# A transformer block with gated delta rule: two levels of block products for gate and up of three batches, moved behind all delta rules

## The chip, the cores and the metric

The kernel runs on one core of one Trainium2 chip, all in fp32. The metric is device microseconds of one execution; lower is better. Three runs of the kernel before are at hand, and one execution was profiled.

## The reference

One adaLN block over x of 4 batches, 512 tokens and 512 channels:

```python
h = _layernorm(x) * (1 + ca) + sa
x = x + ga * attn(h)          # gated delta rule, 6 heads, key 64, value 128
h = _layernorm(x) * (1 + cb) + sb
x = x + gb * ffn(h)
# attn: q, k, v = silu(conv4(h @ W)); beta = sigmoid(h @ Wb); g = -exp(A) * softplus(h @ Wa + dt)
#       per token: S *= exp(g); S += k (v - k S) * beta; o = q S
#       then rmsnorm(o) * silu(h @ Wg) @ Wo
# ffn:  (silu(h @ w_gate.T) * (h @ w_up.T)) @ w_down.T,  512 -> 2048 -> 512
```

`sa, ca, ga, sb, cb, gb` come from a small product of the conditioning vector of each batch.

## The kernel before

One program, written as Python that emits instructions; a list scheduler then sets the order on each engine by priority (the order of emission, with some work put later by `tc.high_priority(-LATER)`). The stages per batch b:

- `normed_t`, `keys`, `queries`, `values`, `gates`: layer norm, transposes and projections (L424), with the convolutions. Batch 0 comes first by itself, the others together.
- `triangles(b)`: for each chunk of 64 tokens a triangular system is inverted. The 64x64 key products (L574) are weighted and stored in DRAM, come back as `pm` with one system to a partition, and DVE substitutes forward in 60 dependent operations (`tip` L598, `ti` L602). The inverses go out to DRAM again (`td`, `ttd`, L606 and L607), and `operands` (L609) loads them for the delta rule (L651 to L653).
- `delta_rule(b)`: four steps of `operands`, `scan` (L682, products L704), `finish` (L717), `project` (L735, L745) and `turned` (L759). `turned` makes the normalised, transposed input of the feed-forward (`hf`), by transposes into `pxn` and ACT. In this kernel `hf` stays in SBUF, two batches at a time.
- `feed_forward(b)` (L814). Tokens are split in halves, and so are channels, so that gate and up of a pair of feature blocks are 2x2 block products, made by seven products instead of eight: `two_blocks` (L947) with matmuls of 128x128 by 256 columns (L960) and sums by ACT and DVE (L965 to L974). The four differences of the tokens (`hs`) are made once in a batch on DVE, and the sums of the weights once for all batches by POOL in `weight_sums` (L794), into DRAM (`wsum`). Silu (L989) and the product with up (L990) give `hid`. A quarter is two such pairs, 512 of the 2048 features. Its down projection is direct (`down`, L842 and L847, 128x512; DVE multiplies by `gb`, L852, POOL adds to the residual, L853) or by seven products (`down_by_seven`, L871 and L890) in quarters 1 to 3 of batch 2 and 0 to 2 of batch 3: POOL makes the left factors (`left_factors`, L857), and the sums of the down weights (`dsum`) were made in feed-forward 1. `seven_to_output` (L903 to L931) ends a batch; its steps are let out one by one by `some`.

PSUM has banks `fill` (3) and `seq` (3). Loads go through SP's queue; DMA issues of one queue are in the order of the schedule. The stages around the change are emitted in this order:

```python
triangles(2)
feed_forward(0)
delta_rule(2)
triangles(3)
feed_forward(1)
delta_rule(3)
feed_forward(2)
feed_forward(3)
```

Since a feed-forward stands between the triangles and the delta rule that reads them, it runs beside the substitution on DVE. A quarter's down follows one pair later than its gate and up, and the last quarter of feed-forwards 0 to 2 is pending into the stage that follows.

Of the kernel before, what the change touches and what calls it, by code (L numbers as in the profile page):

```python
# [15 lines left out]
P = 128  # L16
# [6 lines left out]
S = 32  # L23
# [10 lines left out]
LATER = 4000  # L34


@with_exitstack
def adaln_block(
# [29 lines left out]
    w1 = ctx.enter_context(tc.tile_pool(name="w1", bufs=1))  # L68
    stage_b = ExitStack()
# [9 lines left out]
    def fill(name):  # L79
        return bank("fill", 3, name)  # L80
# [10 lines left out]
    def seq(name):  # L91
        return bank("seq", 3, name)


    kd, qd, vd, sd, gd, xmid = ([] for _ in range(6))
    for b in range(B):
        kd.append(dr.tile([P, NP, T], F32, name=f"kd{b}"))
        qd.append(dr.tile([P, NP, T], F32, name=f"qd{b}"))
        vd.append(dr.tile([NT, P, H, DV], F32, name=f"vd{b}"))
        sd.append(dr.tile([NT, DV, H, P], F32, name=f"sd{b}"))  # L100
        gd.append(dr.tile([2, 2, H, NT, C + 1], F32, name=f"gd{b}"))
        xmid.append(dr.tile([T, D], F32, name=f"xmid{b}"))
    wsum = [dr.tile([NF // 2, P, 7, 2, P], F32, name=f"wsum{i}") for i in range(2)]
# [109 lines left out]
    def load_x(b):  # L213
        ts = []
        if b == 2:

            room = w1.tile([P, NT, D], F32, tag="hf", bufs=2, name=f"xt{b}")
        for c in range(NT):
            if b == 2:
                t = room[:, c, :]  # L220
            else:
                t = pa_.tile([P, D], F32, tag="xt", bufs=4, name=f"xt{b}_{c}")
            (act if b else sp).dma_start(t, x[b, c * P : (c + 1) * P, :])
            ts.append(t)
        return ts
# [298 lines left out]
    ex, at, td, ttd, hf = {}, {}, {}, {}, {}  # L524

    def triangles(b):
# [9 lines left out]
        kp = w1.tile([P, NP, T], F32, tag="kp", bufs=1, name=f"kp{b}")  # L536
# [50 lines left out]
        pm = w1.tile([n, S, S], F32, tag="pm", name=f"pm_{b}")  # L587
        sp.dma_start(pm, ad)
        t = w1.tile([n, S, S], F32, tag="ti", name=f"ti_{b}")
        tmp = w1.tile([n, S * S // 4], F32, tag="tip", name=f"tip_{b}")  # L590
# [168 lines left out]
    def turned(b, c, xn):  # L759
        pt = seq(f"pxn{b}_{c}")  # L760
        for k in range(KD):
            pe.transpose(pt[:, k * P : (k + 1) * P], xn[:, k * P : (k + 1) * P], ident)
        for k in range(KD):
            act.activation(
                hf[b][:, k, c * P : (c + 1) * P], pt[:, k * P : (k + 1) * P], AF.Identity,
                bias=mod_t[:, 2, k, b : b + 1], scale=mod_t[:, 3, k, b : b + 1],
            )

    def delta_rule(b):
        ga = w1.tile([P, D], F32, tag="ga", name=f"ga{b}")  # L770
        sp.dma_start(ga, gate_d[0, b].partition_broadcast(P))
        hf[b] = w1.tile([P, KD, T], F32, tag="hf", bufs=2, name=f"hf{b}")
        st = operands(b, 0)
        for c in range(NT):
            nxt = operands(b, c + 1) if c + 1 < NT else None
            o = scan(b, c, st, nxt)
            finish(b, c, o, ga)
            st = nxt
# [35 lines left out]
    def feed_forward(b):  # L814
        nonlocal pd_

        own = pd_ if b == B - 1 else pc_
        gb = own.tile([P, D], F32, tag="gb", bufs=1, name=f"gb{b}")
        sp.dma_start(gb, gate_d[1, b].partition_broadcast(P))
        xm = []  # L820
        for c in range(NT):
            t = own.tile([P, D], F32, tag="xm", bufs=NT, name=f"xm{b}_{c}")
            sp.dma_start(t, xmid[b][c * P : (c + 1) * P, :])
            xm.append(t)
        ht = hf[b]
# [4 lines left out]
        if more is None:  # L830
            more = own.tile([P, 3, 2, TH], F32, tag="hs", bufs=1, name=f"hs{b}")
# [6 lines left out]
        tdn, acc, left = {}, {}, {}  # L838

        fast = {2: [1, 2, 3], 3: [0, 1, 2]}.get(b, [])  # L840
# [15 lines left out]

        def left_factors(q, j):  # L857

            hid = hids[q, j]
            a11, a12, a21, a22 = (  # L860
                hid[:, k, i * TH : (i + 1) * TH] for i in range(2) for k in range(2)
            )
            t = pd_.tile([P, 3, TH], F32, tag="sd", bufs=4, name=f"sd{b}_{q}_{j}")
            s1, s2, s4 = (t[:, k] for k in range(3))
            pool.tensor_add(s1, a21, a22)
            pool.tensor_sub(s2, s1, a11)
            pool.tensor_sub(a21, a11, a21)
            pool.tensor_sub(s4, a12, s2)
            left[q, j] = a11, a12, a22, a21, s1, s2, s4

        def down_by_seven(q):  # L871


            sums = {}
            for j in range(2):
                a11, a12, a22, a21, s1, s2, s4 = left[q, j]
                wd = wdn[q, j].rearrange("p j (h d) -> p j h d", h=2)
                d1, d2, d4, d3 = (tdn[q, j][:, k] for k in range(4))
                sums[j] = [
                    (a11, wd[:, 0, 0]), (a12, wd[:, 1, 0]), (s2, d2), (s1, d1), (a21, d3),  # L880
                    (s4, wd[:, 1, 1]), (a22, d4),
                ]
            if q == fast[0]:
                acc[0] = pd_.tile([P, 7, 2, 2 * P], F32, tag="acc", bufs=1, name=f"acc{b}")
            for k in range(7):
                o = fill(f"pds{b}_{q}_{k}").rearrange("p (c d) -> p c d", c=2)
                for c in range(2):
                    for j in range(2):
                        l, r = sums[j][k]
                        pe.matmul(o[:, c], l[:, c * P : (c + 1) * P], r, start=j == 0, stop=j == 1)  # L890
                if q == fast[0]:
                    act.copy(acc[0][:, k], o)
                else:
                    vec.tensor_add(acc[0][:, k], o, acc[0][:, k])

        def quarter(q):
            if q not in fast:
                return down(q)
            down_by_seven(q)
            if q == fast[-1]:  # L900
                ending.append(seven_to_output())

        def seven_to_output():  # L903

            p1, p2, p6, p5, p7, p3, p4 = (acc[0][:, k] for k in range(7))

            def add_to(tokens, k, v):
                ds = slice(k * TH, (k + 1) * TH)
                vec.tensor_tensor(v, v, gb[:, None, ds].broadcast_to([P, 2, TH]), ALU.mult)
                for c in range(2):  # L910
                    pool.tensor_add(xm[tokens + c][:, ds], xm[tokens + c][:, ds], v[:, c])

            vec.tensor_add(p6, p6, p1)
            vec.tensor_add(p1, p1, p2)
            yield
            vec.tensor_add(p7, p7, p6)
            add_to(0, 0, p1)
            yield
            vec.tensor_add(p2, p6, p5)
            vec.tensor_add(p2, p2, p3)  # L920
            yield
            vec.tensor_add(p4, p4, p7)
            add_to(0, 1, p2)
            yield
            vec.tensor_add(p5, p5, p7)
            add_to(2, 0, p4)
            yield
            add_to(2, 1, p5)
            if fast[-1] == NQ - 1:
                for i in range(NT):  # L930
                    sp.dma_start(out[b, i * P : (i + 1) * P, :], xm[i])  # L931

        def some(n):
            while ending and n:
                n -= 1
                if next(ending[0], 1):
                    ending.clear()
# [9 lines left out]
        def two_blocks(o, n, src, i):  # L947
# [6 lines left out]
            def product(l, r):  # L954
                count[0] += 1
                if count[0] % 2 == 0:
                    some(1)
# [18 lines left out]
        for i in range(0, NF, 2):  # L976
# [3 lines left out]
            wd = own.tile([P, 2, D], F32, tag="fwd", bufs=2, name=f"wdn{b}_{i}")  # L980
# [11 lines left out]
            if i == (0 if b == B - 1 else 2):  # L992
                complete()
                if b == 2:
                    stage_b.close()
                    pd_ = ctx.enter_context(
                        tc.tile_pool(name="pd", bufs=2, side="right", reuse_waits="tile")
                    )
            if b == 1:
# [9 lines left out]
            if q in fast:  # L1009
                tdn[q, j] = pd_.tile([P, 4, 2 * P], F32, tag="td", bufs=4, name=f"td{b}_{q}_{j}")  # L1010
                sp.dma_start(tdn[q, j], dsum[i // 2])
                left_factors(q, j)
            if j == 0 and q > 0:
                quarter(q - 1)
        if b == 2:
            pending.append(lambda: quarter(NQ - 1))
        else:
            some(9)
            quarter(NQ - 1)


    pd_ = None
    ending, count = [], [0]
# [38 lines left out]
    pc_ = ctx.enter_context(tc.tile_pool(name="pc", bufs=2, reuse_waits="tile"))  # L1062
# [6 lines left out]
    feed_forward(0)  # L1069
    delta_rule(2)  # L1070
    triangles(3)
    feed_forward(1)
    delta_rule(3)
    feed_forward(2)
    feed_forward(3)
# [45 lines left out]
```

## Time and profile before

| | us |
|---|---|
| median of 3 runs | 1312.97 |
| lowest, highest | 1311.42, 1314.52 |
| span of the profiled execution | 1315.2 |
| PE busy | 1234.9 (94%) |
| DVE busy | 733.7 (56%) |
| ACT busy | 383.5 (29%) |
| POOL busy | 290.8 (22%) |

The profiled execution is one of its own; its span stands 2.2 us above the median of the runs. In 40 slices of the span, each digit the tenths of it in which an engine is busy (PEclk: the granted clock of TensorE):

```profile
PE   6799898999889998999999999799999999999998
DVE  3665865656188255784445558543555543563564
POOL 4100214533210012030023121233111221131113
PEclk9799898999899999999999999899999999999999
```

A group of instructions is named by line, engine, operation and tile, then busy us in all, mean ns of one, and idle time before them with what ended it. Every fp32 matmul makes two records.

### The profile page before, as it was taken

The page shows a single profiled execution, that of the slowest core. Times are in us where ns is not written, and L with a number is a line of the kernel's source. Part 1 is how long each engine was busy: PE and PEld are TensorE (multiplying, and loading weights), DVE is VectorE, ACT ScalarE, POOL GpSimd, SP SyncE. Part 2 cuts the span into 40 slices and gives each one's busy share as a digit, 9 for nine tenths or more (in the row PEclk, how much of TensorE's full clock was granted, in tenths as well). Part 3 has the DMA queues.
Part 4 walks back from the last instruction along what each step waited for, and adds up shares of the span by engine and source line. Part 5 has one row for each costly group of instructions (what it writes and reads, how often), then busy time and mean ns, then how long its engine had stood idle before and what let it go on. Part 6 is the DMA issues. An engine that isn't in the chain of part 4 may idle for free.

```text
span 1315.2 us, 18413 instructions
## 1 busy us (share of the span) xinstructions
PE 1234.9 (94%) x6752; PEld 807.1 (61%) x6752; DVE 733.7 (56%) x1574; ACT 383.5 (29%) x740; POOL 290.8 (22%) x357
## 2 busy tenths in 40 slices
PE   6799898999889998999999999799999999999998
PEld 3345355554344565767757666666666578888884
DVE  3665865656188255784445558543555543563564
ACT  2633355554142354211103332101134312112110
POOL 4100214533210012030023121233111221131113
PEclk9799898999899999999999999899999999999999
DMA  7579667667874537664436555544632555444431
GB/s 209 138 203 288 186 173 209 172 212 249 255 205 126 144 98 176 199 202 139 134 113 189 124 126 165 161 130 150 193 85 70 174 186 175 146 152 152 140 114 62
DMA packets 217945, 214.57 MB, mean 163 GB/s; under 512 B 95608, under 2 KB 164216, under 8 KB 217856
## 3 DMA queue, kind: packets, MB, share of 16 engines
q1 hardware_dynamic: 194976, 176.58, 46.4%
q10 hardware_dynamic: 19360, 17.93, 4.2%
q0 software_dynamic: 3520, 18.89, 3.8%
q8 instruction: 54, 0.88, 0.3%
q14 instruction: 35, 0.29, 0.1%
HBM read 159.23 MB, written 50.97 MB: 160 GB/s over the span
## 4 chain that ended last, share of the span: by engine, by line
PE 64%; DVE 14%; DMA 11%; POOL 5%; issue 3%; ACT 2%; SPq 1%; POOLq 0%; DVEq 0%; ACTq 0%
PE phg L960 14%; PE phu L960 11%; PE pd L847 9%; PE pwo L745 5%; PE pds L890 4%; PE pp_v L424 3%; PE pp_g L424 3%; PE pm L704 2%; DVE ti L602 2%; PE scratch L631 2%; DMA wsum<-wsg 2%; DVE tip L598 2%; DMA wsum<-wsu 2%; PE pp_q L424 1%; PE pp_k L424 1%
## 5 line engine op out<-in xcount | busy, mean ns | idle before, releaser
L847 PE MATMUL pd<-wdn,hid 128*128 128x512 f32 x320 | 140.6, 592 | 0.0
L960 PE MATMUL phg<-hf,wg 128*128 128x256 f32 x512 | 138.4, 387 | 1.8 <-DMA wg<-wsum 1.8
L960 PE MATMUL phg<-hs,wg 128*128 128x256 f32 x384 | 103.6, 390 | 5.9 <-DVE hid L967 5.8
L960 PEld LDWEIGHTS phg<-hf,wg 128*128 128x128 f32 x512 | 95.9, 192 | 20.7 <-issue 6.3
L960 PE MATMUL phu<-hf,wu 128*128 128x256 f32 x384 | 101.1, 388 | 2.2 <-DMA wu<-wsum 2.0
L847 PEld LDWEIGHTS pd<-wdn,hid 128*128 128x128 f32 x320 | 60.7, 190 | 68.1 <-issue 63.6
L960 PE MATMUL phu<-hs,wu 128*128 128x256 f32 x384 | 95.6, 382 | 2.5 <-DVE up L973 2.5
L424 PE MATMUL pp_g<-ht,wg 128*128 128x512 f32 x192 | 91.6, 617 | 5.7 <-DMA wg<-in_w_g_dram 4.6
L853 POOL TENSOR_TENSOR xm<-xm,tmpf 128x512 f32<-128x512 f32 x40 | 50.9, 1273 | 206.8 <-DVE tmpf L852 206.8
L424 PE MATMUL pp_v<-ht,wv 128*128 128x512 f32 x192 | 89.3, 609 | 3.5 <-DVE v L503 2.3
L745 PE MATMUL pwo<-wo,ot 128*128 128x512 f32 x192 | 91.8, 608 | 0.0
L965 ACT COPY hid<-phg 128x256 f32<-128x256 f32 x32 | 11.9, 372 | 247.9 <-PE phg L960 247.9
L960 PEld LDWEIGHTS phg<-hs,wg 128*128 128x128 f32 x384 | 71.5, 193 | 20.4 <-DVE hid L967 8.3
L960 PEld LDWEIGHTS phu<-hs,wu 128*128 128x128 f32 x384 | 71.9, 191 | 19.2 <-DVE up L973 7.1
L960 PEld LDWEIGHTS phu<-hf,wu 128*128 128x128 f32 x384 | 71.7, 192 | 15.5 <-issue 3.1
L424 PEld LDWEIGHTS pp_g<-ht,wg 128*128 128x128 f32 x192 | 35.1, 195 | 43.0 <-issue 41.8
L852 DVE TENSOR_TENSOR tmpf<-pd,gb 128x512 f32<-128x512 f32 x40 | 27.5, 689 | 59.4 <-PE pd L847 44.7
L424 PEld LDWEIGHTS pp_v<-ht,wv 128*128 128x128 f32 x192 | 35.2, 193 | 41.5 <-issue 38.5
L989 ACT ACTIVATE hid<-hid 128x1024 f32<-128x1024 f32 x32 | 33.8, 1057 | 86.2 <-DVE hid L973 70.0
L434 DVE SCALAR_TENSOR_TENSOR acc_v<-pp_v,conv_v,acc_v 128x511 f32<-128x511 f32 (+2 forms) x72 | 53.4, 743 | 9.8 <-ACT acc_v L432 8.8
L704 PE MATMUL pm<-r,l 128*128 128x128 f32 x384 | 53.8, 285 | 1.0 <-ACT r L700 0.9
L704 PEld LDWEIGHTS pm<-r,l 128*128 128x128 f32 x384 | 48.2, 194 | 8.9 <-ACT r L700 4.7
(244 smaller groups left out, 2060.1 us busy)
## 6 DMA issues: line engine op xcount, KB each, us to landing
wdn<-in_w_down_t_dram SPq DMA_DIRECT2D x32, 512.0 KB, 4.3
wg<-wsum SPq DMA_DIRECT2D x32, 512.0 KB, 3.8
wu<-wsum SPq DMA_DIRECT2D x32, 512.0 KB, 3.6
wg<-wsum SPq DMA_DIRECT2D x32, 384.0 KB, 4.4
wu<-wsum SPq DMA_DIRECT2D x32, 384.0 KB, 4.3
wsum<-wsg POOLq DMA_DIRECT2D x8, 896.0 KB, 4.3
wsum<-wsu POOLq DMA_DIRECT2D x8, 896.0 KB, 4.6
vd<-v SPq DMA_DIRECT2D x24, 256.0 KB, 3.4
```

What stands on the lines that cost most here:

```text
L424: pe.matmul(pp, w[:, k, :], ht[:, k, :], start=(k == 0), stop=(k == KD - 1))
L434: vec.scalar_tensor_tensor(acc[:, i:], pp[:, : T - i], taps[:, col, TAPS - 1 - i : TAPS - i], acc[:, i:], ALU.mult, ALU.add,)
L598: vec.tensor_tensor(v, pm[:, j, j + 1 :, None].broadcast_to([n, m, j]), t[:, j : j + 1, :j].broadcast_to([n, m, j]), ALU.mult,)
L602: vec.tensor_add(t[:, j + 1 :, :j], t[:, j + 1 :, :j], v)
L704: pe.matmul(pm[:, h], l[:, hs.start + h, 2 * par : 2 * par + 2, :], r[:, par, hs.start + h], start=True, stop=True,)
L745: pe.matmul(pw, ot[:, h, :], wo[:, h, :], start=(h == 0), stop=(h == H - 1))
L847: pe.matmul(pd, hids[q, i // 2][:, i % 2, c * P : (c + 1) * P], wdn[q, i // 2][:, i % 2, :], start=(i == 0), stop=(i == NQ - 1),)
L852: vec.tensor_mul(tmp, pd, gb)
L853: pool.tensor_add(xm[c], xm[c], tmp)
L890: pe.matmul(o[:, c], l[:, c * P : (c + 1) * P], r, start=j == 0, stop=j == 1)
L960: pe.matmul(o, l[:, k], r[:, k], start=k == 0, stop=k == 1)
L989: act.activation(hid, hid, AF.Silu)
```

## The change

- The order becomes `triangles(2)`, `delta_rule(2)`, `triangles(3)`, `feed_forward(0)`, `delta_rule(3)`, then a `tail` for batches 1, 2 and 3. `feed_forward` is for batch 0 alone now (one level, direct down), and makes `dsum`.
- `turned` stores its result in DRAM (`hd[b]`, one store to each of four token blocks), and feed-forward 0 and the tail load it from there.
- `moving` makes the token side of both levels: the tokens are in blocks of 128, 12 DVE differences to a batch give 7 x 7 operands.
- `two_level` (called for the gate by `quarter_of`, which ends with one silu of 2048 columns) makes gate (or up) of a quarter, 512 features: the first level's seven weight sums are loaded from `wsum` in two halves (four, then three of them), POOL makes the second level's sums of them (four operations to a half), then seven groups of products of 128x128 by 128 columns, summed by ACT and DVE, and the sums of the first level in SBUF (three or four DVE operations). The last product of each half is deferred (`settle`) into the next half. The weight tiles and the sums have two buffers each.
- `down_of` (called through `late`, one quarter later) makes every down of the tail by seven products, but the last quarter of batch 3, which is direct.
- `kp`, `pm`, `ti`, `tip` lie in a pool of their own that is closed before the tail; the load of batch 2's x has a tile of its own.

```diff
@@ turned
+        h = w1.tile([P, KD, P], F32, tag="hf", bufs=2, name=f"hf{b}_{c}")
         for k in range(KD):
             act.activation(
-                hf[b][:, k, c * P : (c + 1) * P], pt[:, k * P : (k + 1) * P], AF.Identity,
+                h[:, k, :], pt[:, k * P : (k + 1) * P], AF.Identity,
...
+        sp.dma_start(hd[b][:, :, c * P : (c + 1) * P], h)
@@ two_level(o, n, src, q, yz, then)
+        for s, m0, nm in ((0, 0, 4), (1, 4, 3)):
+            ms = slice(m0, m0 + nm)
+            w = pc_.tile([P, 2, 4, 2, P], F32, tag="fw", bufs=2, name=f"w{nn}")[:, :, :nm]
+            e = pc_.tile([P, 3, 4, P], F32, tag="fe", bufs=2, name=f"e{nn}")[:, :, :nm]
+            for a in range(2):
+                sp.dma_start(w[:, a], src[2 * q + a][:, ms])
+            x11, x12, x21, x22 = (w[:, a, :, k] for a in range(2) for k in range(2))
+            s1, s2, s4 = (e[:, j] for j in range(3))
+            pool.tensor_add(s1, x21, x22)
+            pool.tensor_sub(s2, s1, x11)
+            pool.tensor_sub(x21, x11, x21)
+            pool.tensor_sub(s4, x12, s2)
...
+            products(ba, x11, y11, True)
+            act.copy(p1, ba)
+            products(bb, s1, t1, True)
+            act.copy(p5, bb)
+            settle()
+            some(1)
+            products(ba, s2, t2, False)
+            act.copy(u2, ba)
+            bc = view(seq(f"pc{nn}"))
+            products(bc, x12, y21, True)
+            vec.tensor_add(c11, bc, p1)
+            products(bb, s4, y22, False)
+            vec.tensor_add(c12, bb, u2)
+            products(ba, x21, t3, False)
+            vec.tensor_add(c22, ba, p5)
+
+            def ending_(s=s, part=part, products=products, ba=ba, x22=x22, t4=t4, c21=c21):
+                products(ba, x22, t4, False)
+                act.copy(c21, ba)
+                v = [o[:, :, j] for j in range(4)]
+                if s == 0:
+                    vec.tensor_add(v[1], v[1], v[0])
+                    vec.tensor_add(v[2], v[2], v[0])
+                    vec.tensor_add(v[0], v[2], v[3])
+                else:
+                    r = [part[:, :, j] for j in range(3)]
+                    vec.tensor_add(v[2], v[2], r[0])
+                    vec.tensor_add(v[3], v[3], v[2])
+                    vec.tensor_add(v[0], v[0], r[1])
+                    vec.tensor_add(v[2], v[2], r[2])
+                    then()
+            left_over.append(ending_)
@@ tail(bs): for each batch and quarter
+                h = quarter_of(b, q, yz)
...
+                if late:
+                    late()
...
+                two_level(
+                    u, f"u{b}_{q}", wsum[1], q, yz,
+                    lambda u=flat[0], h=flat[1]: vec.tensor_mul(u, u, h),
+                )
+                late = lambda b=b, q=q, u=u, held=held: down_of(b, q, u, held, b == bs[-1])
@@ down_of
+        pool.tensor_add(s1, a21, a22)
+        pool.tensor_sub(s2, s1, a11)
+        pool.tensor_sub(a21, a11, a21)
+        pool.tensor_sub(s4, a12, s2)
...
+        for k, l in enumerate((a11, a12, s2, s1, a21, s4, a22)):
+            o = seq(f"pds{b}_{q}_{k}").rearrange("p (c d) -> p c d", c=2)
+            for c in range(2):
+                for a in range(2):
+                    pe.matmul(o[:, c], l[:, 2 * a + c], right[a][k], start=a == 0, stop=a == 1)
...
+            if k == 0:
+                settle()
@@ order
 triangles(2)
-feed_forward(0)
 delta_rule(2)
 triangles(3)
-feed_forward(1)
+feed_forward(0)
 delta_rule(3)
-feed_forward(2)
-feed_forward(3)
+stage_c.close()
+stage_t.close()
+pc_ = ctx.enter_context(tc.tile_pool(name="pe", bufs=2, reuse_waits="tile"))
+tail(list(range(TAIL, B)))
```

## The prediction

> **What bounds the kernel now.** I began with busy time by engine and the chain of work that ended last, then took the groups of instructions, and went to single stretches for the stages that the change touches.
>
> ```profile
> span 1315.2 us, 18413 instructions
> PE 1234.9 (94%) x6752; PEld 807.1 (61%) x6752; DVE 733.7 (56%) x1574; ACT 383.5 (29%) x740; POOL 290.8 (22%) x357
> ...
> PE 64%; DVE 14%; DMA 11%; POOL 5%; issue 3%; ACT 2%; SPq 1%; POOLq 0%; DVEq 0%; ACTq 0%
> ```
>
> TensorE is busy for 94% of the span and carries 64% of the chain: fewer or shorter matmuls shorten the kernel wherever nothing new makes them wait. The chain, row by row (start, length, what), gives the speed of a dense run:
>
> ```profile
> 578.09 11.16 PE pd L847 x26
> 589.25 6.04 PE phg L960 x28
> ...
> 616.37 11.16 PE pd L847 x26
> ...
> 1085.91 9.93 PE pds L890 x46
> 1095.84 6.04 PE phg L960 x28
> ```
>
> Every fp32 product is two records. A record of 512 columns takes 11.16/26 = 0.429 us, one of 256 columns 6.04/28 = 0.2157. From 578.09 to 616.37 is one quarter of a feed-forward (two i-pairs of gate and up, and a direct down): 38.3 us; with a down by seven products the period is 37.0 (1085.91 to 1122.87). In these stages PE is the only bound. Where it is not, the stretches say:
>
> ```profile
> 540.00:560.00 20.00, 20.00 (x88) 16.86 (x88) 18.33 (x55) 5.43 (x10) 0.00 (x0) 0.95 0.77 244
> 560.00:580.00 20.00, 17.46 (x71) 12.66 (x71) 19.42 (x44) 5.71 (x9) 4.92 (x3) 1.00 0.72 213
> 820.00:840.00 20.00, 16.02 (x60) 13.15 (x60) 16.05 (x38) 2.81 (x6) 8.72 (x11) 0.83 0.49 149
> 840.00:860.00 20.00, 16.20 (x58) 11.86 (x58) 7.17 (x17) 2.17 (x4) 0.00 (x0) 0.91 0.45 137
> ```
>
> (Columns: busy us of PE, weight loads, DVE, ACT, POOL, then granted clock, DMA share, GB/s.) From 540 to 580 DVE works all the time on the triangle inverses of batch 2 (L598/L602), and PE is still full: feed-forward 0 covers them. That cover is what the change moves.
>
> **The change, part by part.** I work on the profiled span, 1315.2; the median of the three runs is 2.2 below it, and I take that off at the end.
>
> *1. PE work, removed.* A quarter of gate and up in one level is 2 x 2 x 7 x 2 products of 256 columns, 112 records x 0.2157 = 24.16 us. In two levels it is 2 x 49 products of 128 columns, 196 records. The nearest row is the 128-column product of the delta rule:
>
> ```profile
> 464.54 1.53 PE pm L704 x12
> ...
> L704 PE MATMUL pm<-r,l 128*128 128x128 f32 x384 | 53.8, 285 | 1.0 <-ACT r L700 0.9
> ```
>
> Single records inside those bursts start 0.1115 apart. Ends: 0.107 (half of the 256-column one) and 0.1275 (1.53/12, tail counted): 21.0 to 25.0 us a quarter. I take the start-to-start distance: 21.85, a gain of 2.31, in 12 quarters 27.7. Five more quarters go from the direct down (32 x 0.429 = 13.73) to seven products (56 x 0.2157 = 12.08): 8.2. Together 35.9 less.
>
> *2. The inverses of batch 2 lose their cover.* Now delta rule 2 follows them at once. Their input has landed at 540.5 in the trace of before; the copy is 1.1, the 60 dependent operations with their gaps 21.2, three scans (L541) 3.6 and four differences 2.7 that sit ahead on DVE. The store is issued near 569.3, and in batches 0 and 1 the first product that uses it comes 7.6 to 7.9 later: 577. PE is done with delta rule 1 at 537.6 and has 17 matmuls of feed-forward 0 to fill in (7.3 us). So some 32 us stand idle. Bounds: 25 (the scans and differences run in earlier gaps) to 36.
>
> *3. Feed-forward 0 and delta rule 3.* First product to last transpose was 101.7, 103.5 and 102.7 in batches 1 to 3; I keep 102 to 577+102 = 679. What is left of feed-forward 0 between the delta rules is 102.4 us of dense PE. Loads queued on SP behind the store of the inverses cost 8 to 10, as at 820 to 860 (the clock 0.83 and 0.91, PE 16 of 20): delta rule 3 begins near 791. Into it come the first POOL sums and 12 DVE differences (4 x 0.69, 4 x 0.69, 4 x 0.5): I add 5 (0 to 10) to 102, which makes 898.
>
> *4. The tail.* From there PE has 391.9 us of work (the whole of batches 1 to 3, 408.8, less 16.9 that lies inside delta rule 3), and the last quarter's chain of sums ahead of the direct down, and the output, leave about 12: 1302 if PE never waits. It will. Per quarter the rows are:
>
> ```profile
> wg<-wsum SPq DMA_DIRECT2D x32, 512.0 KB, 3.8
> ...
> L867 POOL TENSOR_TENSOR hid<-hid 128x256 f32<-128x256 f32 x12 | 9.8, 815 | 0.0
> L853 POOL TENSOR_TENSOR xm<-xm,tmpf 128x512 f32<-128x512 f32 x40 | 50.9, 1273 | 206.8 <-DVE tmpf L852 206.8
> L919 DVE TENSOR_TENSOR acc<-acc 128x512 f32<-128x512 f32 x2 | 1.4, 680 | 0.0
> L916 DVE TENSOR_TENSOR acc<-acc 128x512 f32<-128x512 f32 x2 | 2.4, 1186 | 0.1
> ```
>
> Weight buffers are two, and each half of a gate or an up takes one. The load of the next gate's first half can start only when the product D of the up's first half has ended. Counted from that up's first product: 24 products are issued by 5.35, D (deferred into the second half) ends at 7.6, the second half at 10.26. The load lands 3.7 later, so A1 begins at 11.6 where PE was free at 10.26. The other 512 KB are there at 13.1; only then do four dependent POOL sums start (1.27 each): the first at 14.4, the second at 15.7 to 16.1, the fourth at 18.2 to 19.6, and product B2 waits for it. Behind B2 on PE's queue stand A3, the next half and everything after. Without collision of DVE and POOL that is 3.7 of waiting; with it, 5 in this half alone. Then the products of the down wait for up, which waits for a copy, four DVE adds (0.69) and a multiplication of 2048 columns (2.4, twice the 1.22 to 1.25 of L990), and POOL makes the down's left factors (4 x 1.27) in the same queue as the sums of the next weights.
>
> The collision is in the rows. L916 and L919 are the same operation on the same shape: 680 ns alone, 1186 beside a POOL operation; L972 is 423 alone and 828 to 834 beside POOL; POOL's L867 goes from 725 to 900. A pair so met (0.69 with 1.27) takes about 1.7 together, not 1.27. DVE operations that read PSUM show no such stretch. POOL has 8 x 1.27 + 8 x 1.0 + 4 x 1.27 = 23.2 us a quarter; DVE's operations with both operands in SBUF are 14 x 0.69 + 2.4 = 12.1, of which about 8.5 is not hidden in those pairs: 32 us for the two together, against 33.9 of PE (21.85 + 12.08), and they are chained through each other. So a quarter is 37.7 (no collision) to about 42, the wait s per quarter 3.7 to 8; I take 6 between these, nearer to the collided rows. 12 x 6 = 72.
>
> The Trainium skill, "SBUF — State Buffer", section "Who interferes with whom", has a harder rule: a DVE operation with two SBUF inputs and a GpSimd one that reads SBUF exclude each other for the whole instruction. By it a pair takes 0.69 + 1.27 = 1.96; an estimate with 14 such pairs adds 3.4 a quarter, 40 in all. The rows show some overlap, so I keep theirs. The same skill's "TensorE: Matmul & The Clock Gate", "What's actually happening", says that an idle window of about 3.4 us halves the clock until one busy window has passed; by it each wait as long as B2's would cost up to 1.7 more (estimate), 20 over 12 quarters. The trace shows lower clocks only behind far longer gaps, at 820 to 860.
>
> *Sum.* 898 + 391.9 + 12 + 72 = 1374 of span; the same from the other side: 1315.2 - 35.9 + 32 + 72 - about 8 (waits that the old feed-forwards had) = 1375. Less 2.2: **1372 us**, about 4.5% slower. With s from 3.7 to 8 and the bounds of 2 and 3: 1335 to 1407.
>
> **Rivals.** *A. The waits are small.* The POOL sums are ready earlier than I count because products C and the deferred D lie ahead of B1, and the loads land in 3.5: s of 0.5 to 3.5, so 1306 to 1342. For it: 38 us periods show that loads of this size hide today. Against it: today a buffer holds a whole two-block step and no sum stands between landing and product.
>
> *B. Faster.* The inverses' hole and the waits together stay under the 35.9 that PE saves. That needs one mechanism: the POOL sums always end before PE reaches B1, so that s is 1 or less and the PE's saving shows undiminished: 1302 + 12 - 2 - the 5 of delta rule 3 = 1307 at s = 1, 1285 if the hole is also only 20. It decides from s = 1.2 downward (with 5 less in delta rule 3). Against it: load after D, then four serial sums, is 5 us longer than the PE work beside it.
>
> *C. No gain on PE, or harder collisions.* At 0.1275 a record (weight loads for every 128 columns: PEld has 194 ns records of its own, one to each product) gate and up cost 25.0 a quarter, 38 more, less what then hides of s; or s is 8 to 11. 1407 to 1440.
>
> *D. The order alone decides*: the tail costs nothing, but the hole of 32 cancels the 36: within 0.2%.
>
> **How the numbers follow.** The forecast (s about 6, own range 1335 to 1407): 0.57. A, from 1316 up: 0.16. C: 0.17. B, with the faster end of A: 0.08. D: 0.02. Measurements of this kernel tell about 0.2% (2.6 us) from no change, so faster 0.08, same 0.02, slower 0.90. The range leaves out B and D, the lower part of A and the upper part of C: 1322 to 1420.
>
> **What would show it.** In the changed kernel: a hole of 25 to 36 us in PE between delta rules 1 and 2, ended by the inverses' store and load; quarter periods of 38 to 42 between equal products of the tail, with PE records of 128 columns 0.11 apart; waits of PE ended by POOL's sums (second weight sum, fourth sum) and by the load of gate weights; DVE adds of 512 columns at 1.1 to 1.2 us beside 0.68. Wrong would be: records 0.125 or more apart (C), or periods of 34 to 35 (B), or a full PE from 540 to 580.

## The result and the profile after

The changed kernel takes 1467.76 us (median of 4 runs, 1457.65 to 1475.11) against 1313.74 before on the same chip: a ratio of 1.1166 [1.1114, 1.1218], slower by 11.7%. I had forecast slower by 4.5%, 1372 us, range 1322 to 1420. The sign is right, the size is not, and the time lies outside the range. The profiled execution, the shortest of the four, has a span of 1455.9; 1374 was expected.

The page after, the lines that answer those of before:

```profile
span 1455.9 us, 21304 instructions
## 1 busy us (share of the span) xinstructions
PE 1240.7 (85%) x7880; PEld 865.6 (59%) x7880; DVE 921.1 (63%) x1581; ACT 451.3 (31%) x830; POOL 578.7 (40%) x533
...
PE   6799989989899954999899997778878888877886
...
POOL 4100235332000213021333244546777567765582
PEclk9899999999999976999999989999999999999999
...
PE 45%; DVE 27%; DMA 11%; POOL 8%; issue 5%; ACT 3%; SPq 1%; POOLq 0%; ACTq 0%; DVEq 0%
```

PE's share of the chain falls from 64 to 45% and DVE's doubles. PE's row has a hole in slices 15 and 16 (the inverses of batch 2), and runs at seven to eight tenths from slice 25 on, the tail. POOL's busy time has doubled, nearly all of the increase there.

The hole in the chain of waits, after:

```profile
533.46 4.00 DMA pm<-ad
...
569.68 2.96 DMA td<-ti
572.71 3.97 DMA t<-td
577.65 1.29 PE phu L876 x6
578.95 0.81 PE scratch L663 x22
```

The store is at 569.7, the inverses land again at 576.7, and the first product that reads them starts at once, at 576.73 in the timeline (in the chain its other 22 records stand at 578.95): 569.3 and 577 had been worked out.

One inner quarter of the tail, 1187.57 to 1230.40, in the chain of waits (the load of the gate's first half, its four POOL sums, and the products behind the fourth):

```profile
1195.86 4.52 DMA wg<-wsum
...
1200.52 1.28 POOL eg L968
...
1201.86 1.60 POOL eg L969
1203.46 1.67 POOL wg L970
1205.13 1.68 POOL eg L971
...
1206.85 2.08 PE pbg L991 x8
1208.93 2.14 PE pag L991 x14
```

The seven groups of products are named by their bank in PSUM, the memory that products are written to (`pa`, `pb`, `pc`), in the order of the code A1, B1, A2, C, B2, A3 and the deferred D. Counted from the up's first product, the gate's A1 started at 11.7, B1 at 14.3, A2 at 15.9 and B2 at 19.3 (the timeline); worked out were 11.6, 14.4, 15.7 to 16.1 and 18.2 to 19.6. The eight records of B2 start 0.23 apart and the fourteen behind them 0.16, where 0.1115 is the dense pace. Two short stretches say why (columns as in the prediction: PE, weight loads, DVE, ACT, POOL, granted clock, DMA share, GB/s):

```profile
1202.00:1206.80 4.80, 2.38 (x18) 2.00 (x18) 4.77 (x4) 1.17 (x2) 4.80 (x4) 0.98 0.48 164
1206.80:1211.00 4.20, 4.15 (x23) 4.15 (x24) 4.06 (x3) 0.00 (x0) 4.12 (x2) 0.62 0.00 0
```

PE was busy for half of 4.8 us, with no gap over 2.0, and after that its mean clock was 0.62 over 4.2 us. In the tail the clock's record falls to 0.5 eleven times, for 44.4 us together, and seven of the eleven times no gap over 2.05 stands in the 3.4 us ahead. The kernel before shows the same on a small scale: behind a gap of 1.99 (846.78 to 848.77) it ran at half the clock.

```profile
845.70:849.12 3.42, 1.44 (x8) 0.98 (x7) 1.53 (x4) 1.06 (x1) 0.00 (x0) 1.00 0.90 291
849.12:852.54 3.42, 3.42 (x10) 2.71 (x9) 0.00 (x0) 0.37 (x1) 0.00 (x0) 0.50 0.89 277
```

To add such losses up I took the distance from each matmul record to the next: what exceeds 0.1115, 0.2157 or 0.429 (128, 256, 512 columns) by more than 0.35 us counts as a wait, the rest of the excess as slow running (lower clock and small waits together). What is left is the work at the dense pace, by this reckoning the predicted 33.93 us in every inner quarter. That the pace is right the records show: in the two quarters from 1144.84 to 1230.40 the median distance of 128-column records of one group is 0.112.

| stretch of the changed kernel | length | PE work | waits | slow running |
|---|---|---|---|---|
| delta rule 2 (577.0 to 683.1) | 106.1 | 99.4 | 5.9 | 0.8 |
| feed-forward 0 (to 795.4) | 112.3 | 103.2 | 6.6 | 2.5 |
| delta rule 3 (to 916.8) | 121.4 | 96.7 | 19.0 | 5.7 |
| tail (to the end) | 539.1 | 391.6 | 110.1 | 31.8 |
| an inner quarter of the tail | 42.7 to 44.4 | 33.9 | 6.2 to 8.0 | 1.7 to 2.8 |
| a quarter at the turn of a batch | 45.0 to 50.2 | 33.9 | 6.7 to 13.9 | 2.5 to 4.8 |

An inner quarter is the second or third of a batch, from the first product of its up to that of the next; batch 1's second, 53.7, is counted with the first quarters. Of the tail's length 5.6 us lie behind its last product. Before, delta rule 3 (940.4 to 1043.3) was 102.9 with waits of 3.9 and slow running of 2.9, and a dense quarter had waits of 0 to 0.4.

The price of DVE and POOL beside each other, by shape, in the tail of the changed kernel:

```profile
L1024 DVE TENSOR_TENSOR up<-up,partu 128x512 f32<-128x512 f32 x12 | 20.0, 1663 | 0.0
...
L970 POOL TENSOR_TENSOR wg<-wg 128x512 f32<-128x512 f32 x11 | 18.9, 1715 | 0.0
...
L1119 POOL TENSOR_TENSOR sd<-sd,up 128x512 f32<-128x512 f32 x11 | 14.0, 1272 | 0.8
...
L1018 DVE TENSOR_TENSOR up<-up 128x512 f32<-128x512 f32 x12 | 8.2, 684 | 0.0
```

The same DVE shape takes 684 ns with no POOL sum beside it (the twelve of L1018) and 1663 in the mean where POOL's sums run (eleven of L1024's twelve take some 1750). The same POOL shape takes 1715 in such a stretch and 1272 at L1119; fourteen sums of this shape that no DVE operation touches take 1259 to 1282.

### The profile page after: what moved, and what is told of

Read it like the earlier page. It is cut to its first block, busy times and chain, and to the rows that moved or that the text cites. A ratio compares the mean times of both kernels' runs of the same rounds, so it can differ in the third digit from the quotient of the medians.

```text
span 1455.9 us, 21304 instructions
## 1 busy us (share of the span) xinstructions
PE 1240.7 (85%) x7880; PEld 865.6 (59%) x7880; DVE 921.1 (63%) x1581; ACT 451.3 (31%) x830; POOL 578.7 (40%) x533
## 4 chain that ended last, share of the span: by engine, by line
PE 45%; DVE 27%; DMA 11%; POOL 8%; issue 5%; ACT 3%; SPq 1%; POOLq 0%; ACTq 0%; DVEq 0%
PE pwo L749 5%; DMA wg<-wsum 3%; PE pp_v L428 3%; PE pd L848 3%; PE pau L991 3%; PE pag L991 3%; PE pp_g L428 3%; PE phu L876 3%; PE phg L876 2%; PE pds L1135 2%; DVE tip L602 2%; DVE ti L606 2%; PE pm L708 2%; PE pp_k L428 2%; DMA wsum<-wsu 2%
## 5 line engine op out<-in xcount | busy, mean ns | idle before, releaser
L968 POOL TENSOR_TENSOR eg<-wg 128x512 f32<-128x512 f32 (+1 forms) x24 | 31.7, 1322 | 146.3 <-PE pag L991 93.8
L991 PE MATMUL pag<-y,wg 128*128 128x128 f32 x336 | 51.9, 307 | 18.3 <-DMA wg<-wsum 18.3
L428 PEld LDWEIGHTS pp_v<-ht,wv 128*128 128x128 f32 x192 | 35.9, 196 | 44.7 <-issue 41.8
L438 DVE SCALAR_TENSOR_TENSOR acc_v<-pp_v,conv_v,acc_v 128x509 f32<-128x509 f32 (+2 forms) x72 | 53.3, 743 | 11.5 <-ACT acc_v L436 10.6
L991 PEld LDWEIGHTS pag<-y,wg 128*128 128x128 f32 x336 | 46.6, 217 | 21.6 <-issue 17.7
L848 PE MATMUL pd<-wdn,hid 128*128 128x512 f32 x128 | 59.0, 601 | 0.0
L876 PE MATMUL phg<-ht,wg 128*128 128x256 f32 x128 | 37.1, 412 | 23.6 <-DMA wg<-wsum 23.0
L749 PEld LDWEIGHTS pwo<-wo,ot 128*128 128x128 f32 x192 | 34.9, 196 | 33.1 <-issue 30.1
L1135 PE MATMUL pds<-td,up 128*128 128x256 f32 x176 | 45.0, 401 | 10.7 <-ACT acc L1137 10.7
L428 PE MATMUL pp_q<-ht,wq 128*128 128x512 f32 x96 | 50.3, 658 | 0.0
L428 PE MATMUL pp_k<-ht,wk 128*128 128x512 f32 x96 | 45.4, 607 | 3.7 <-DMA wk<-in_w_k_dram 2.5
L969 POOL TENSOR_TENSOR eg<-eg,wg 128x512 f32<-128x512 f32 (+1 forms) x24 | 46.9, 1954 | 1.7
```

The costliest lines, as they stand in the source:

```text
L428: pe.matmul(pp, w[:, k, :], ht[:, k, :], start=(k == 0), stop=(k == KD - 1))
L438: vec.scalar_tensor_tensor(acc[:, i:], pp[:, : T - i], taps[:, col, TAPS - 1 - i : TAPS - i], acc[:, i:], ALU.mult, ALU.add,)
L749: pe.matmul(pw, ot[:, h, :], wo[:, h, :], start=(h == 0), stop=(h == H - 1))
L848: pe.matmul(pd, hids[q, i // 2][:, i % 2, c * P : (c + 1) * P], wdn[q, i // 2][:, i % 2, :], start=(i == 0), stop=(i == NQ - 1),)
L876: pe.matmul(o, l[:, k], r[:, k], start=k == 0, stop=k == 1)
L968: pool.tensor_add(s1, x21, x22)
```

## The experiments

My theory after the result: the order costs the hole, and the tail's waits come from load, then POOL's sums, made longer by collisions with DVE's sums and paid again in PE's clock. Rivals: DVE's own sums are the bound; the load alone; the order spoils delta rule 3 by itself. All ratios are to the kernel before, on the same chip.

| kernel | median us | ratio [95%] | inner quarter |
|---|---|---|---|
| changed | 1467.8 | 1.1166 [1.1114, 1.1218] | 42.7 to 44.4 |
| order alone, one-level tail | 1359.3 | 1.0329 [1.0272, 1.0387] | dense |
| without POOL's second-level sums | 1375.7 | 1.0495 [1.0414, 1.0575] | 37.0 to 37.2 |
| without DVE's first-level sums | 1408.5 | 1.0716 [1.0660, 1.0772] | 40.8 to 41.6 |
| three weight buffers | 1433.1 | 1.0898 [1.0845, 1.0952] | 39.5 to 41.4 |
| old order, tail of two batches | 1412.0 | 1.0765 [1.0714, 1.0815] | 43.5 to 44.0 |
| ready operands in 14 buffers | 1357.9 | 1.0346 [1.0307, 1.0384] | 36.1 |
| the same, old order, two batches | 1344.8 | 1.0245 [1.0200, 1.0291] | 36.1 |
| without the inverses of batch 2 | 1458.3 | 1.1063 [1.0994, 1.1132] | as changed |
| delta rule 3 finished first | 1479.0 | 1.1207 [1.1129, 1.1286] | 43.2 to 44.8 |
| tail from batch 3 | 1486.7 | 1.1311 [1.1271, 1.1351] | 42.7 to 43.7 |

**Order alone.**

```diff
     delta_rule(3)
+    feed_forward(1)
+    feed_forward(2)
+    feed_forward(3)
...
-    tail(list(range(TAIL, B)))
...
```

> The new order with the old one-level feed-forwards for batches 1 to 3 as well, all downs direct (no two-level tail). Theory (the order costs the uncovered inverses, the rest is the tail's): 1313 + 32 for the hole + 9.9 for six quarters that lose their down by seven products (6 x 1.65), so 1345 to 1362, with the hole between delta rules 1 and 2 at 570 to 577 us and dense quarters of 38 us afterwards. Rival (the order also spoils delta rule 3 by itself): over 1365, with delta rule 3 at 115 to 121 us instead of 102 to 104.

Within the theory's range: 45.7 more than before, of which 9.9 were worked out for the direct downs, so the order, with the tokens' way through DRAM that it keeps, costs some 36 (the interval of the ratio is 8 us either way). Delta rule 3 took 118 us as the rival has it, but with 110 us of PE work in it and 8 of waits and slow running: it is longer because more work of the feed-forwards stands in it (some 96 before), not spoiled.

**Without POOL's sums.**

```diff
-            s1, s2, s4 = (e[:, j] for j in range(3))
-            pool.tensor_add(s1, x21, x22)
-            pool.tensor_sub(s2, s1, x11)
-            pool.tensor_sub(x21, x11, x21)
-            pool.tensor_sub(s4, x12, s2)
+            s1, s2, s4 = x11, x12, x22
```

> Leaves out POOL's sums of the second level in the tail (products use the loaded blocks in their place). Theory (load, then four serial POOL sums, and their collision with DVE, make most of the tail's waits): inner quarters fall from 42.8 to 43.8 to 36 to 38, delta rule 3 loses some 5 to 10 of its 121, total 1360 to 1395. Rival 1 (DVE's own sums are the bound): inner quarters stay at 40 to 42, total 1425 to 1445. Rival 2 (load of the weights is what counts): 40 to 41, since the load of 3.4 us is still waited for.

The theory's range, in the quarters and in the total. Two inner quarters of this kernel, and all that PE waited for in them:

```profile
1096.60:1170.90 74.30, 70.22 (x505) 65.28 (x505) 45.86 (x67) 21.25 (x35) 10.01 (x8) 1.00 0.45 157
```

```profile
PE pag L986 <- DMA wg<-wsum: 2.2, 2, 1.2
PE pds L1130 <- DVE up L1064: 1.3, 2, 0.6
PE pag L986 <- DVE partg L1005: 0.6, 2, 0.3
```

The same two quarters of the changed kernel:

```profile
1144.84:1230.40 85.56, 73.67 (x506) 67.11 (x504) 61.16 (x67) 21.29 (x35) 56.74 (x40) 0.98 0.37 127
```

```profile
PE pbg L991 <- POOL eg L971: 3.9, 2, 2.0
PE pag L991 <- DVE partg L1010: 3.6, 2, 2.1
PE pag L991 <- DMA wg<-wsum: 2.2, 2, 1.2
PE pag L991 <- POOL eg L969: 1.0, 2, 0.5
```

The wait for the load stays to the tenth (2.2). The waits for POOL go, and so does most of the one for DVE's subtotal (3.6 to 0.6), and DVE's busy time in the two quarters falls from 61.2 to 45.9 although it has the same 67 operations: that difference, 15.3, is what POOL's company had cost DVE. Slow running falls from 1.7 to 2.8 a quarter to 0.67: it was a consequence of the waits, not a cause of its own.

**Without DVE's sums.**

```diff
                 if s == 0:
-                    vec.tensor_add(v[1], v[1], v[0])
...
-                    vec.tensor_add(v[2], v[2], r[2])
+                if s == 1:
                     then()
```

> Leaves out the seven DVE sums of the first level between two SBUF operands in each gate and up of the tail; POOL's sums stay. Theory: without collisions the POOL chain ends 1.3 us earlier in each gate and the product that waits for DVE's last subtotal (1.6 to 2.2) goes, up is ready earlier: inner quarters 39 to 40.5, total 1405 to 1430. Rival 1 (DVE is the bound): inner quarters 35.5 to 37, total 1365 to 1385.

The total is the theory's; the quarters, 40.8 to 41.6, lie just above its 39 to 40.5 and far from the rival's 35.5 to 37. POOL's sums alone keep a wait of 2.9 to 3.5 in each inner quarter, now at B1, the product of the first sum. DVE is not the bound.

**Three weight buffers.**

```diff
-            w = pc_.tile([P, 2, 4, 2, P], F32, tag="fw", bufs=2, name=f"w{nn}")[:, :, :nm]
+            w = pc_.tile([P, 2, 4, 2, P], F32, tag="fw", bufs=3, name=f"w{nn}")[:, :, :nm]
...
-                    own = pc_ if (b - bs[0]) % 2 == 0 else pd_
+                    own = pc_
...
```

(`fwd` moves to the other pool as well.)

> Three weight buffers instead of two in the tail; to make room, the token operands of all three batches share one buffer, which lengthens only the quarters at the start of batches 2 and 3 (some 5 to 12 us each). Theory: the gate's load can start about 5 us earlier, so that the waits for the load (1.2 to 1.5) and for the second and fourth POOL sum (2.6 to 3.3) go from inner quarters: 38 to 39.5, total 1415 to 1445. Rival 1 (DVE and its collisions): inner quarters 42 or more, total 1460 to 1485.

The total is in the theory's range, the quarters only by half. The waits for the load and for POOL's sums are gone from inner quarters, as the theory has it. In three of the six slow running is down to 0.8 and the period is 39.5; the others took 41.2 to 41.4, with 2.3 of slow running. What is waited for now is DVE (the multiplication that ends up, and the subtotals). A load one buffer earlier is worth 2 to 4 us a quarter.

**Old order, two batches.**

```diff
-TAIL = 1
+TAIL = 2
...
 triangles(2)
+feed_forward(0)
 delta_rule(2)
 triangles(3)
-feed_forward(0)
+feed_forward(1)
 delta_rule(3)
```

> The order of before (feed-forward 0 between the inverses of batch 2 and delta rule 2, feed-forward 1 between those of batch 3 and delta rule 3), the two-level tail for batches 2 and 3 alone. Theory (hole 32, and a two-level batch costs 27 more than one of one level with direct downs): 1466 - 32 - 27 = 1407, range 1395 to 1430; the hole between delta rules 1 and 2 is gone, delta rule 3 keeps its 15 to 18 of added waits, inner quarters stay at 42.8 to 44. Rival (the hole was no cost, since the work that fills it now is missing later): 1435 or more.

In range (1412), with the inner quarters as expected; the hole is gone. The gain over the changed kernel by the ratios is 53, where 59 was worked out.

**Ready operands, in the new and in the old order.**

```diff
-            w = pc_.tile([P, 2, 4, 2, P], F32, tag="fw", bufs=2, name=f"w{nn}")[:, :, :nm]
-            e = pc_.tile([P, 3, 4, P], F32, tag="fe", bufs=2, name=f"e{nn}")[:, :, :nm]
...
+            for j in range(7):
+                t = pc_.tile([P, 4, P], F32, tag="fw", bufs=14, name=f"w{nn}_{j}")[:, :nm]
+                sp.dma_start(t.rearrange("p m t -> p (m t)"), ...)
+                ch.append(t)
+            x11, s1, s2, x12, s4, x21, x22 = ch
```

> The changed order, but the tail loads all seven second-level operands of each half as if they lay ready in DRAM (7/4 of the bytes; the data are other parts of the first-level sums, so the values differ), in 14 small buffers that come free one by one, without POOL's sums. Theory (what is left of the waits then is the load behind the last deferred product): inner quarters 35 to 36.2, down from 37.0 to 37.3 without the sums alone, slow-clock share under 1 us a quarter, total 1345 to 1365. Rival (the bytes, some 8 MB a quarter, arrive too late): 37.5 or more, total 1380 or more.

> The same tail of ready operands for batches 2 and 3 alone, with the order of before. Theory (two batches of 142 instead of 148 to 151, the start of a batch and delta rule 3 some 4 to 8 longer each): 1295 to 1318, so about the time of before or up to 1% less; this bounds what two levels can bring when the sums cost nothing. Rival (start of batches and delta rule 3 eat more than that): 1320 to 1345.

The first holds: 1357.9, 36.1 a quarter, no wait for any load in inner quarters although the transfers rise from 157 to 236 GB/s:

```profile
1096.60:1168.70 72.10, 69.76 (x505) 65.19 (x504) 45.95 (x67) 21.26 (x35) 10.00 (x8) 1.00 0.70 236
```

The second fails on the rival's side: 1344.8. Quarters of 36.1 are shorter than the 37.0 to 38.3 of before, yet the kernel is 32 slower. From the end of delta rule 1 on (799 us against 777 in the traces), PE's waits are 59 us against 25 (the other 7 us between the two traces lie ahead of that point): 15.5 in delta rule 3 (3.9 before), 23.0 behind it (4.4 before; about 8 of them in the last quarter ahead of the last direct down, which waits for up's sums and a multiplication of 2048 columns, and 1 a quarter at the first product of the seven-product down), and 9.0 in feed-forward 0 (2.7 before), most of them for sums that DVE has still to make beside the inverses. The new places of waiting outweigh what the quarters gain. So even with sums that cost nothing, two levels as they are staged here do not beat one. I ran no version that does.

**Without the inverses of batch 2.**

```diff
-            for j in range(1, S - 1):
+            for j in range(1, S - 1) if b != 2 else ():
```

> The changed kernel without the 60 dependent substitution operations of batch 2 (its inverses are left out, so batch 2's values differ). Theory (they stand uncovered between delta rules 1 and 2): 21 us of the hole go and nothing gives them back, 1466 - 21 = 1445, range 1437 to 1453; first product of delta rule 2 near 557 instead of 578.9. Rival (the loads of the delta rule or the transfers end last there anyway): under 8 us gained.

My theory fell. Delta rule 2 did start 29 us earlier (first product at 547.5, 576.7 in the changed kernel), but delta rule 3 ended at 914.4, where the changed kernel has 916.8, and the profiled spans are 1455.2 and 1455.9. The ratios put the gain at 14, with 11 either way, so the size is open between the two expectations. Stretches of this kernel:

```profile
535.00:577.00 42.00, 23.71 (x241) 18.27 (x241) 13.59 (x32) 9.95 (x28) 3.04 (x3) 0.64 0.46 117
577.00:683.00 106.00, 92.88 (x644) 64.60 (x645) 66.50 (x154) 37.08 (x79) 26.54 (x24) 0.93 0.67 183
683.00:795.00 112.00, 111.20 (x422) 76.78 (x420) 54.54 (x121) 13.02 (x27) 35.71 (x42) 1.00 0.46 155
```

and of the changed one:

```profile
535.00:577.00 42.00, 12.88 (x41) 9.64 (x41) 34.21 (x78) 7.78 (x12) 8.46 (x9) 0.56 0.73 233
577.00:683.00 106.00, 101.04 (x878) 69.85 (x878) 57.96 (x136) 40.78 (x93) 20.66 (x18) 1.00 0.53 136
683.00:795.00 112.00, 106.15 (x388) 72.31 (x388) 66.95 (x147) 15.19 (x30) 35.54 (x41) 0.98 0.47 152
```

The first stretch gains 11 us of busy PE, but 18 us of waits stay in it: 8.9 for the load of the inverses, some 4 at delta rule 1's last transposes, the rest in delta rule 2's own chain, which now runs without feed-forward 0's products between its own. The second has 17 us of waits (5.9 in the changed kernel), about half of them delta rule 2's and half those of feed-forward 0's products, and a clock of 0.93. The third has 1 us (6.6). From 535 to the end of delta rule 3 PE's waits are 57 us, where the changed kernel has 62. So the inverses' duration is not the order's cost of 36: most of it stays as gaps of delta rule 2 and of what follows it.

**Delta rule 3 by itself.** First with the delta rule's last steps emitted ahead of the tail (`complete()` before its loop), then with the tail's batches in the order 3, 1, 2 as well.

> The changed kernel with delta rule 3 finished before the tail is begun. Theory (delta rule 3 takes 121 instead of 102 since products of the tail stand in PE's queue ahead of its own and wait there for ACT and DVE): delta rule 3 falls to 98 to 106, the tail gets some 17 us of products and the start of the first gate (differences, loads, POOL sums, 15 to 25 us without PE) back; total 1466 to 1490. Rival (delta rule 3 is longer for another reason, its own loads or what the feed-forward left pending): it stays over 112.

The total is in range, but the scheduler still put 66 records of the tail ahead of the last transpose, and delta rule 3 took 116: the edit did not make the separation that it was for, so it tells nothing.

```diff
+        complete()
         late = None
...
-    tail(list(range(TAIL, B)))
+    tail([3, 1, 2])
...
```

> The changed kernel with delta rule 3 finished and the tail in the order 3, 1, 2: batch 3's tokens exist only after delta rule 3, so that no product, sum or difference of the tail can stand beside it, as some still could with the stages merely finished in order. Theory (the tail's 12 differences and first sums, 26 us of DVE and 21 us of POOL between 795 and 917, lie in the queues that delta rule 3's chain goes through): first product to last transpose of delta rule 3 in 96 to 106 instead of 121; total 1465 to 1495, since the tail's start gets bare. Rival (delta rule 3 is longer for want of filling work or through its own loads): still 112 or more.

Delta rule 3 took 112.6 (797.6 to 910.2), 9 less than in the changed kernel and still the rival's 112 or more. PE's work in it is only 80 us (97 in the changed kernel), and its waits are 25 (19.0). Against my text, eight POOL sums of the tail's first weights still ran there (835 to 844), since they need no tokens. So of the 18.5 by which delta rule 3 grew, about 9 go when the tail's products and DVE sums, 17 us of PE's work, are taken out of it. For the other half the candidates are the lower clock (0.89 here, 1.00 before), the pending direct down (none stood in delta rule 3 before) and those POOL sums, and which of them it is stays open.

## Why the prediction was wrong

The step that failed is the wait of the tail, s = 6 in each of twelve quarters and nothing for a slower PE. Of the 82 us between the two spans, 63 are the tail's; the time lies above the range of every rival too.

*1. PE work, 35.9 less: right.* Records of 128 columns start 0.112 apart (0.1115 was taken), and with ready operands a whole quarter took 36.1, little above the 33.93 of work that was worked out. Rival C's first half falls. (The weight loads that it named are one to each record, not to each product: PE and PEld have the same 6752.)

*2. The hole, 32: right in place and length, and about right in price.* PE's waits from 530 to 577 are 34.4, and the order alone cost some 36. The reason was too narrow: I priced the inverses, and without them most of the loss stays, as gaps of delta rule 2 and behind it.

*3. The stages to delta rule 3: 795.4 for 791.* Delta rule 3 itself was put at 107 and took 121.4. I had counted POOL sums and differences as 5, and not that products of the tail on PE's queue wait there for ACT and DVE: some 8 of its 19.0 us of waits stand at such products (2.9 for one copy by ACT). What made the rest is open.

*4. The tail: this term failed.* Expected were 391.9 of work, 72 of waits in twelve quarters of s = 6, and 12 at the end: 476. Measured are 539.1: 391.6 of work, 110.1 of waits, 31.8 of slow running, 5.6 behind the last product. Of the waits 5.8 stand ahead of the last direct down, so that the 12 at the end are 11.4; the other 104 are 32 more than the 72, and the slow running is as much again. Four parts of it:

- The recurrence up to B2 was right (19.3 for 18.2 to 19.6), and the waits of inner quarters, 6.2 to 8.0, are near 6. What it lacked was the wait behind B2: the next half's deferred D needs a bank that DVE has read (L1010), and DVE is held up there by POOL's left factors of the down: 1.4 to 2.1 a quarter.
- I took one s for all quarters. At the turn of a batch the waits are 6.7 to 13.9. In the worst, from 1275.45, the steps of the output stand on DVE ahead of up's subtotals, and D waits for these. The gate's load, which can start only behind D, starts 10.3 us after up's first product (8.3 in the inner quarter above) and takes 6.4 to land (3.4), with loads of the residual and stores of the output beside it:

```profile
PE pag L991 <- DMA wg<-wsum: 4.9, 1, 4.9
PE pds L1135 <- ACT acc L1137: 2.2, 1, 2.2
```

- In the first two quarters the waits are 13.0 and 14.5 (those of the first in part beside delta rule 3). No output of the tail is pending there. The longest wait, in the quarter from 952, is that of a product of the first down by seven products. It needs a bank that ACT has copied (L1137); the copy stands behind the gate's silu (L1041), and the silu waited for DVE, which makes batch 2's differences between the gate's sums:

```profile
PE pds L1135 <- ACT acc L1137: 6.8, 1, 6.8
ACT L1041 <- DVE hid L1025: 8.1, 1, 8.1
```

- Slow running, which I put at nothing. Quarters without POOL's sums have 0.67 of it; the tail has 31.8 in all, some 24 more than that rate gives. Its 44.4 us at half the clock can cost at most 22 of them.

The prediction set aside the Trainium skill's "TensorE: Matmul & The Clock Gate", "What's actually happening", because the trace showed lower clocks only behind far longer gaps. That reading of the trace was wrong: at 849.12, inside the very stretch that it named, the clock falls behind a gap of 1.99. The estimate by the page was 20 over the tail, and about 24 were measured. In kind the page was the better guide. In its letter it isn't met: that section asks for an idle window of some 3.4 us, and here gaps of 2.0 and less in 4.8 us of half-busy PE were followed by a clock of 0.62. For the collisions the rows were the better guide than the skill's "SBUF — State Buffer", "Who interferes with whom": by exclusion for whole instructions a pair would take 1.96, and in the chain above POOL's sums, with a DVE sum beside each, follow each other every 1.67 (1203.46, 1205.13), where 1.7 was taken.

Of the rivals, C's second half came nearest (s of 8 to 11, 1407 to 1440): the waits and slow running of the tail over twelve quarters are 11.8 each, the end included. A and B had the waits hidden; a tail without POOL's sums shows what that would have been worth. (B's 1285 is a slip: 1307 less the 12 by which the hole would be shorter is 1295.)

## What to carry to other kernels

A finer block product can pay only if its operands and sums leave no wait: count, for every product, load plus sums against the PE work that stands beside them with the buffers there are, and do it for the first and last pieces of a batch separately. Small waits that left PE half busy cost again in its clock here, so a sum of waits was a lower bound. What the reorder uncovered was not one operation's length but all gaps that the moved work had filled.

## What the runs showed of the hardware

- Matmuls of 128x128 by 128 columns in fp32 start 0.112 us apart per record (median of two quarters of the tail), two records to a product, each record with its own weight load; with ready operands (36.1 us a quarter) these loads caused no wait.
- The granted clock fell to 0.62 over 4.2 us after PE had been busy for 2.38 of 4.8 us, with no single gap over 2.0. Its drops to one half last 3.41 us or a multiple of it. I cut the twelve traces, from 80 us on, into windows of that length in step with the drops. 4255 of the windows were at full clock. All 140 of them in which PE was busy for less than 42% were followed by half the clock; from 42 to 61% it was 56 of some 230, above 61% one.
- A DVE sum of two SBUF operands (0.684 alone) and a POOL sum (1.27 alone) that run in each other's company take 1.67 a pair.
- Loads of seven operands a half, at 236 GB/s and a DMA share of 0.70, caused no wait in an inner quarter.
